# One batch's turned input by transfers, separations on a second engine, last products in two banks, a new order

## The chip, the cores and the metric

The kernel runs on one core of a Trainium2 chip. The core has a matrix engine (TensorE, PE in the profile), a vector engine (VectorE, DVE), an activation engine (ScalarE, ACT), a general engine (GpSimd, POOL), and a sync engine (SyncE, SP) that here only issues DMA transfers. The metric is the device time of one execution in microseconds (us). Lower is better. The time before is the median of three runs.

## The reference

Four batches of 256 rows and 512 columns go through four layers. Cut to what matters:

```python
# L0, x: (4, 256, 512)
w = softmax(x @ router_W.T + router_b)              # (4, 256, 8)
a_sum = einsum('bsh,arh->bsr', x, ctx)              # the context is lora_A
upd = einsum('bsn,bsnh->bsh', w, einsum('bsr,nhr->bsnh', a_sum, lora_B))
x = nan_to_num(x + 0.5 * upd, posinf=1e4, neginf=-1e4)
# L1, cross attention with 32 heads of 16, then a layer norm
Q = x @ Wq.T + bq; K = ctx @ Wk.T + bk; V = ctx @ Wv.T + bv
attn = softmax(where(mask, Q K^T / 4, -inf))
x = layernorm(x + (attn V) @ Wo.T + bo) * ln_g + ln_b
# L2 and L3, each four blocks; the 8 nearest of 512 points from ctx
for i in range(4):
    p = leaky_relu(x)
    x = (w_center[i] p + sum over the 8 neighbours of w_neighbor[i] p) / 9 + x
```

In L2 and L3 both weights are the same matrix, so a block is one product with the weights (`wp`) and one product with a 0/1 matrix that has a one for each neighbour and one for the point itself (`nbr`, four tiles of 128 x 512 for a batch). There are eight such blocks for each batch, one after the other.

## The kernel before

All work of a batch is cut into steps for one engine each. `mixture(b)` is L0, `values(b)`, `queries(b)` and `attention(b, l, ...)` are L1 (`l` is one of the two halves of 128 rows), `nearest(b)` finds the neighbours, and `block(b, i)` is one of the eight blocks. TensorE does all products. A product in full single precision is two instructions in the profile (a transpose is one); in `block` the product `wp` is split into a high and a low part (`wph` by ScalarE at line 1034, `wpl` by VectorE at line 1037), and the product with `nbr` (line 1052) runs over both.

No loop sets the order. The class `Plan` collects every step with an estimated cost, what it reads and writes, and which buffers it needs. `Plan.emit` then plays a list scheduler while the program is built: for each engine it takes, among the steps that could start first (within 0.05 us), the one with the lowest rank. The rank of a step is the due time of its batch (`DEADLINES`) less the length of the work that follows it. A step may have a second engine (`other`); the scheduler takes the one that it thinks ends first. The order found is fixed in the program. Each engine then runs its list in order, and so does the SP queue, where a transfer that waits for its input holds back all transfers behind it. Keys such as `("last", h)` or `after` bind the scheduler alone; what an engine waits for in the run follows from the tiles.

A matmul needs its operand turned, with the contracted dimension on the partitions. `turn(...)` (line 461 and after) does this in two ways. With `by_transfer` false, TensorE transposes four 128 x 128 tiles into a PSUM bank (line 467) and ScalarE copies the bank to SBUF (line 471). With `by_transfer` true, the 32-bit numbers are separated into their upper and lower 16 bits by ScalarE (line 477, tile `..._a`), a DMA transpose issued by SP turns them (line 487, tile `..._t`), and ScalarE or GpSimd joins the halves again (line 495). Three things are turned: `z` (the mixed terms, two for a batch), `x1T` (the updated `x`, two for a batch) and `pT` (the attention weights, eight for a batch). `FROM = 2` says that `z` and `x1T` go by transfer from batch 2 on; `FROM_P = 1` says so of `pT` from batch 1 on.

`mix(b, l, zb)` turns `z`, multiplies it with `lora_BT` (line 523), adds to `x` (line 538), replaces non-finite values (lines 544 to 554), turns the result into `x1T` (line 555), and then adds the bias `bo` to `x` (line 564). The queries of a batch (`q`, line 818) read both halves of its `x1T`. `values` is `v` at line 780.

The loads are issued by SP in the order of the `load...` calls (lines 300 to 324), and they land in that order. `load_xT(3)` is placed in the plan behind the first half of `x1T` of batch 1 (`after`, line 280).

The last block of batch 3 ends in `last(...)`: the second half of its rows is done in two column halves, so that the first half can be added and stored while the second is multiplied. Both column halves are in one PSUM bank, `pb[o]`, and the two additions (line 1107) come after both products (line 1090).

Of the kernel before, what the change touches and what calls it, by code (L numbers as in the profile page):

```python
# [14 lines left out]
ALU = mybir.AluOpType  # L15
# [16 lines left out]
DEADLINES = (0.0, 35.0, 60.0, 67.0)  # L32
# [8 lines left out]
FROM, FROM_P = 2, 1  # L41
# [23 lines left out]
class Plan:  # L65
# [39 lines left out]
    def emit(self, deadline):  # L105
# [16 lines left out]
        while ready:  # L122
# [45 lines left out]
            op.end += op.lag  # L168
# [13 lines left out]
def xattn_seq_kernel(ctx: ExitStack, tc: tile.TileContext, a: dict, out: bass.AP):  # L182
# [106 lines left out]
    def load_k(o):  # L289
        load(("WkT", o), 0.25, lambda: WkT[o], a["WkT"][:, bass.ts(o, H)])  # L290
# [10 lines left out]
    load("cxx2", 0.13, lambda: cxx0[64:128], a["ctx"][0])  # L301
    load("small", 0.05, lambda: consts, a["small"])
    load("ctxT", 0.5, lambda: ctxT.rearrange("p c b v -> p (c b v)"), a["ctxT"])
    load_k(0)
    load_k(2)
    load_points(1)
# [8 lines left out]
    load_x(1)  # L315
    load("rows1", 0.5, lambda: rows1, a["rows1"].partition_broadcast(128))
    load("mask_i", 0.12, lambda: mask_i.rearrange("p b v -> p (b v)"), a["mask"].partition_broadcast(128))
    load_x(2)
    load_w("WoT")
# [141 lines left out]
    def turn(name, by_transfer, src, reads, dst, writes, into=()):  # L461

        if not by_transfer:
# [11 lines left out]
        act(  # L475
            1.08,
            lambda: A_.copy(  # L477
                apart.tile.bitcast(U16).rearrange("p (t n) -> p t n", t=2),
                src().bitcast(U16).rearrange("p (n t) -> p t n", t=2),
            ),  # L480
            reads,
            (apart,),
        )
# [24 lines left out]
    def mix(b, l, zb):  # L508
# [4 lines left out]
            b >= FROM,  # L513
# [5 lines left out]
        for h in range(2):  # L519
# [33 lines left out]
        act(0.63, lambda: A_.activation(odd.tile, v, AF.Identity, bias=zero, scale=0.0), (key, "zero"), (odd,))  # L553
# [3 lines left out]
            b >= FROM,  # L557
# [80 lines left out]
    def nearest(b):  # L638
# [4 lines left out]
        for j in range(H // 128):  # L643
# [11 lines left out]
                0.62,  # L655
# [342 lines left out]
    def block(b, i):  # L998
# [45 lines left out]
        pb = [Buf("bank", f"blk{b}_{i}_{o}") for o in range(NL)]  # L1044

        for m2 in range(2):
            for o in range(NL):

                def gather(m2=m2, o=o):
                    for m in (2 * m2, 2 * m2 + 1):  # L1050
                        for k, part in enumerate(parts[m2]):
                            T_.matmul(  # L1052
                                pb[o].tile,
                                lhsT=part.tile[:, bass.ds(m % 2 * S + o * 128, 128)],
                                rhs=nbr[b, m],
                                start=(m == 0 and k == 0),
                                stop=(m == H // 128 - 1 and k == 1),
                            )

                if (b, i, m2, o) == (B - 1, 2 * NBLK - 1, 1, NL - 1):  # L1060
                    continue
                pe(0.94, gather, (*parts[m2], ("nbr", b, 2 * m2), ("nbr", b, 2 * m2 + 1)), (pb[o],))
        if (b, i) == (B - 1, 2 * NBLK - 1):
            last(b, pb, parts[1], pt)
# [17 lines left out]
    def last(b, pb, parts, pt):  # L1082

        o = NL - 1
        for h in range(2):
            cols = bass.ts(h, H // 2)
            pe(
                0.52,
                lambda cols=cols, h=h: [
                    T_.matmul(  # L1090
                        pb[o].tile[:, cols],
                        lhsT=part.tile[:, bass.ds(m * S + o * 128, 128)],
                        rhs=nbr[b, 2 + m][:, cols],
                        start=False,
                        stop=(h == 1 and m == 1 and k == 1),
                    )
                    for m in range(2)
                    for k, part in enumerate(parts)
                ],
                (*parts, ("nbr", b, 2), ("nbr", b, 3), *pb),  # L1100
                (("last", h),),
            )
        for h in range(2):
# [3 lines left out]
                lambda cols=cols: V_.scalar_tensor_tensor(  # L1107
                    pt[:, o, cols], pb[o].tile[:, cols], 1.0 / (KNN + 1.0), pt[:, o, cols], ALU.mult, ALU.add
                ),
                (pb[o], ("x", b, o), ("last", h)),  # L1110
# [75 lines left out]
```

## Time and profile before

| | |
|---|---|
| median of three runs | 385.94 us (385.63 to 387.9) |
| the profiled execution's own time | 386.5 us |
| its span, first to last instruction | 384.8 us |
| granted TensorE clock | 1.000 |
| TensorE busy | 378.7 us, 98% of the span |
| VectorE busy | 240.0 us, 62% |
| ScalarE busy | 191.3 us, 50% |
| GpSimd busy | 110.3 us, 29% |
| DMA | 25.81 MB, mean 67 GB/s |

The profiled execution took 1.7 us more than its span. Busy time of TensorE counts modelled ends of pipelined matmuls, so 98% says that there is nearly always a matmul under way, not that each runs at its best rate. In a timeline row the first number is the start in us from the beginning of the span and the second how long the group took; then come engine, line, operation, tile written and tiles read, shapes and count; square brackets hold idle time before and who ended it. A row of the groups has the busy time and the mean of one in ns, then the idle time before. A row of the waits has the total in us, how often, and the longest.

### The profile page before, as it was taken

The page shows a single profiled execution, that of the slowest core. Times are in us where ns is not written, and L with a number is a line of the kernel's source. Part 1 is how long each engine was busy: PE and PEld are TensorE (multiplying, and loading weights), DVE is VectorE, ACT ScalarE, POOL GpSimd, SP SyncE. Part 2 cuts the span into 40 slices and gives each one's busy share as a digit, 9 for nine tenths or more (in the row PEclk, how much of TensorE's full clock was granted, in tenths as well). Part 3 has the DMA queues.
Part 4 walks back from the last instruction along what each step waited for, and adds up shares of the span by engine and source line. Part 5 has one row for each costly group of instructions (what it writes and reads, how often), then busy time and mean ns, then how long its engine had stood idle before and what let it go on. Part 6 is the DMA issues. An engine that isn't in the chain of part 4 may idle for free.

```text
span 384.8 us, 5507 instructions
## 1 busy us (share of the span) xinstructions
PE 378.7 (98%) x2120; PEld 291.5 (76%) x2120; DVE 240.0 (62%) x445; ACT 191.3 (50%) x296; POOL 110.3 (29%) x122
## 2 busy tenths in 40 slices
PE   8999999999999999999999999999999999999996
PEld 5848747668887666887867767888888888888885
DVE  1779599995992876955966726535435435435433
ACT  2672755759688769775757722322222221222220
POOL 5483307676356426542054430400000000000000
PEclk9999999999999999999999999999999999999999
DMA  6999500162155305215014610000000001000002
GB/s 201 343 407 348 112 15 1 29 136 42 28 111 112 68 0 110 56 20 90 3 27 89 103 55 2 0 0 2 1 0 2 1 0 56 0 0 2 0 0 111
DMA packets 47386, 25.81 MB, mean 67 GB/s; under 512 B 43200, under 2 KB 43584, under 8 KB 46720
## 3 DMA queue, kind: packets, MB, share of 16 engines
q1 hardware_dynamic: 47360, 25.46, 26.6%
q8 instruction: 17, 0.28, 0.3%
q14 instruction: 9, 0.07, 0.1%
HBM read 12.87 MB, written 2.10 MB: 39 GB/s over the span
## 4 chain that ended last, share of the span: by engine, by line
PE 84%; DVE 9%; DMA 2%; SPq 2%; ACT 2%; issue 1%; DVEq 0%
PE blk L1052 31%; PE wp L1021 29%; PE q L818 7%; PE o L965 5%; PE upd L523 4%; DMA raw<-in_ctx 2%; SPq L273 2%; PE avT L945 2%; PE v L780 1%; PE route L421 1%; PE s L859 1%; DVE rest L649 1%; DVE den L900 1%; DVE s L891 1%; DVE mx L885 1%; DVE top L646 1%
## 5 line engine op out<-in xcount | busy, mean ns | idle before, releaser
L1021 PE MATMUL wp<-fT,p 128*128 128x256 f32 x512 | 120.1, 380 | 0.0
L1052 PE MATMUL blk<-nbr,wph 128*128 128x512 f32 x254 | 110.3, 434 | 0.0
L1021 PEld LDWEIGHTS wp<-fT,p 128*128 128x128 f32 x512 | 96.6, 189 | 17.9 <-issue 2.5
L1052 PE MATMUL blk<-nbr,wpl 128*128 128x512 f32 x254 | 99.6, 392 | 0.0
L1068 DVE SCALAR_TENSOR_TENSOR x<-blk,x 128x512 f32<-128x512 f32 x63 | 42.9, 683 | 69.5 <-PE blk L1052 69.5
L1034 ACT CAST wph<-wp 128x512 fp32r<-128x512 f32 x64 | 37.3, 583 | 94.9 <-PE wp L1021 94.6
L1037 DVE TENSOR_TENSOR wpl<-wp,wph 128x512 fp32r<-128x512 f32 x64 | 43.8, 685 | 37.7 <-ACT wph L1034 37.7
L1052 PEld LDWEIGHTS blk<-nbr,wph 128*128 128x128 f32 x254 | 47.8, 188 | 11.8 <-issue 1.1
L1052 PEld LDWEIGHTS blk<-nbr,wpl 128*128 128x128 f32 x254 | 47.8, 188 | 10.2 <-DVE wpl L1037 0.5
L922 POOL TENSOR_TENSOR s<-s,rden 128x512 f32<-128x512 f32 x32 | 32.6, 1052 | 53.4 <-DVE rden L912 53.4
L1004 ACT ACTIVATE p<-x 128x512 f32<-128x512 f32 x38 | 24.0, 630 | 30.4 <-DVE x L1068 26.6
L477 ACT COPY pT_a<-s 128x1024 uint16<-128x1024 uint16 x24 | 24.6, 1044 | 10.8 <-POOL s L922 6.5
L965 PE MATMUL o<-WoT,avTs 128*128 128x512 f32 x64 | 29.7, 596 | 0.0
L523 PE MATMUL upd<-lora_BT,zTs 128*128 128x512 f32 x64 | 28.8, 597 | 0.8 <-ACT zTs L471 0.8
L818 PE MATMUL q<-x1T,WqT 128*128 128x256 f32 x128 | 29.1, 382 | 0.1
L818 PEld LDWEIGHTS q<-x1T,WqT 128*128 128x128 f32 x128 | 24.0, 190 | 4.0 <-ACT x1T L471 0.6
L523 PEld LDWEIGHTS upd<-lora_BT,zTs 128*128 128x128 f32 x64 | 11.9, 190 | 14.9 <-issue 13.2
L897 ACT ACTIVATE s<-s 128x512 f32<-128x512 f32 x32 | 18.6, 626 | 7.4 <-DVE s L891 7.4
L885 DVE TENSOR_REDUCE mx<-s 128x8 f32<-128x512 f32 x32 | 20.2, 679 | 2.2 <-PE s L859 2.2
L965 PEld LDWEIGHTS o<-WoT,avTs 128*128 128x128 f32 x64 | 11.9, 189 | 11.1 <-issue 10.3
L891 DVE TENSOR_TENSOR s<-s,mx 128x512 f32<-128x512 f32 x32 | 20.2, 678 | 0.0
L900 DVE TENSOR_REDUCE den<-s 128x8 f32<-128x512 f32 x32 | 20.0, 673 | 0.1
(124 smaller groups left out, 415.5 us busy)
## 6 DMA issues: line engine op xcount, KB each, us to landing
xT<-in_xT SPq DMA_DIRECT2D x4, 512.0 KB, 9.7
x<-in_x SPq DMA_DIRECT2D x4, 512.0 KB, 11.2
out<-x SPq DMA_DIRECT2D x7, 256.0 KB, 2.0
WkT<-in_WkT SPq DMA_DIRECT2D x4, 256.0 KB, 6.5
lora_BT<-in_lora_BT SPq DMA_DIRECT2D x1, 1024.0 KB, 9.4
WvT<-in_WvT SPq DMA_DIRECT2D x1, 1024.0 KB, 11.1
rows<-in_rows SPq DMA_DIRECT2D x2, 512.0 KB, 12.3
WoT<-in_WoT SPq DMA_DIRECT2D x1, 1024.0 KB, 11.7
```

What stands on the lines that cost most here:

```text
L477: lambda: A_.copy(apart.tile.bitcast(U16).rearrange("p (t n) -> p t n", t=2), src().bitcast(U16).rearrange("p (n t) -> p t n", t=2),),
L523: T_.matmul(ps2.tile, lhsT=zT.tile[:, bass.ts(c, 128)], rhs=w["lora_BT"][:, c, :], start=(c == 0), stop=(c == NC - 1),)
L818: T_.matmul(ps.tile[:, 0:S], lhsT=w["WqT"][:, c, bass.ts(o, 128)], rhs=x1T[b].tile[:, c, :], start=(c == 0), stop=(c == NC - 1),)
L885: lambda mx=mx, ps=ps: V_.tensor_reduce(mx.tile[:, 0:HPC], heads(ps), AX.X, ALU.max),
L891: lambda mx=mx, ps=ps, s=s: V_.tensor_tensor(heads(s), heads(ps), mx.tile[:, 0:HPC].unsqueeze(2).to_broadcast([128, HPC, V]), ALU.subtract),
L922: lambda s=s, g=g: G_.tensor_tensor(heads(s), heads(s), rden.tile[:, bass.ts(g, HPC)].unsqueeze(2).to_broadcast([128, HPC, V]), ALU.mult,),
L965: T_.matmul(po.tile, lhsT=avT.tile[:, bass.ts(c, 128)], rhs=w["WoT"][:, c, :], start=(c == 0), stop=(c == NC - 1),)
L1021: T_.matmul(ps.tile[:, bass.ts(k, S)], lhsT=p.tile[:, c, bass.ts(2 * m2 + k, 128)], rhs=wi[:, c, :], start=(c == 0), stop=(c == NL - 1),)
L1034: act(0.59, lambda ps=ps, hi=hi: A_.copy(hi.tile, ps.tile), (ps,), (hi,))
L1037: lambda ps=ps, hi=hi, lo=lo: V_.tensor_tensor(lo.tile, ps.tile, hi.tile.bitcast(F32), ALU.subtract),
L1052: T_.matmul(pb[o].tile, lhsT=part.tile[:, bass.ds(m % 2 * S + o * 128, 128)], rhs=nbr[b, m], start=(m == 0 and k == 0), stop=(m == H // 12 ...
L1068: lambda o=o: V_.scalar_tensor_tensor(pt[:, o], pb[o].tile, 1.0 / (KNN + 1.0), pt[:, o], ALU.mult, ALU.add),
```

## The change

- `FROM` is split: `FROM_Z = 2` for `z` as before, `FROM_X = 1` for `x1T`. So both halves of `x1T` of batch 1 are turned by transfers and no longer by TensorE.
- The separation (the first step of a turn by transfer) gets a second engine: ScalarE at an estimated 1.06 us or GpSimd at 1.2 us. This holds for all 34 of them: 24 of `pT`, 4 of `z`, 6 of `x1T`.
- In `last`, the last 128 rows get two banks, `end0` and `end1`, one for each column half. All their products are now done in column halves (16 matmuls of 256 columns, where there were 4 of 512 and 8 of 256), and each addition depends on its own bank.
- The order of the loads: the first quarter of `WkT` and the points of batch 1 come before `ctxT`; the mask and `WoT` come before `rows1`.
- Due times of batches 2 and 3 are 63 and 70 instead of 60 and 67, three estimates of cost are a little different, and a transfer that turns is now taken to land after all loads under way. Estimates and due times change nothing but the order that the scheduler writes.

```diff
-DEADLINES = (0.0, 35.0, 60.0, 67.0)
+DEADLINES = (0.0, 35.0, 63.0, 70.0)
-FROM, FROM_P = 2, 1
+FROM_Z, FROM_X, FROM_P = 2, 1, 1
...
-            op.end += op.lag
+            if op.lag:
+                op.end = max(op.end, self.landed[-1]) + op.lag
...
     load("cxx2", 0.13, lambda: cxx0[64:128], a["ctx"][0])
+    load_k(0)
     load("small", 0.05, lambda: consts, a["small"])
+    load_points(1)
     load("ctxT", 0.5, lambda: ctxT.rearrange("p c b v -> p (c b v)"), a["ctxT"])
-    load_k(0)
     load_k(2)
-    load_points(1)
     load_xT(0)
...
+    load("mask_i", 0.12, lambda: mask_i.rearrange("p b v -> p (b v)"), a["mask"].partition_broadcast(128))
+    load_w("WoT")
     load("rows1", 0.5, lambda: rows1, a["rows1"].partition_broadcast(128))
-    load("mask_i", 0.12, lambda: mask_i.rearrange("p b v -> p (b v)"), a["mask"].partition_broadcast(128))
     load_x(2)
-    load_w("WoT")
...
-        act(
-            1.08,
-            lambda: A_.copy(
+        def split(copy):
+            copy(
                 apart.tile.bitcast(U16).rearrange("p (t n) -> p t n", t=2),
                 src().bitcast(U16).rearrange("p (n t) -> p t n", t=2),
-            ),
+            )
+
+        act(
+            1.06,
+            lambda: split(A_.copy),
             reads,
             (apart,),
+            other=("POOL", 1.2, lambda: split(G_.tensor_copy), True),
         )
...
             f"zT{b}_{l}",
-            b >= FROM,
+            b >= FROM_Z,
...
             f"x1T{b}_{l}",
-            b >= FROM,
+            b >= FROM_X,
...
-    def last(b, pb, parts, pt):
+    def last(b, other, parts, pt):
         o = NL - 1
-        for h in range(2):
+        ends = [Buf("bank", f"end{h}") for h in range(2)]
+        for m2 in range(2):
+            for h in range(2):
...
+                            ends[h].tile[:, 0 : H // 2],
+                            lhsT=part.tile[:, bass.ds(m * S + o * 128, 128)],
+                            rhs=nbr[b, 2 * m2 + m][:, cols],
+                            start=(m2 == 0 and m == 0 and k == 0),
+                            stop=(m2 == 1 and m == 1 and k == 1),
...
-                (pb[o], ("x", b, o), ("last", h)),
+                (ends[h], ("x", b, o)),
```

More of the change, by code (lines that the diff above doesn't have):

```diff
@@ L552, in mix @@
         )
-        act(0.63, lambda: A_.activation(odd.tile, v, AF.Identity, bias=zero, scale=0.0), (key, "zero"), (odd,))
+        act(0.72, lambda: A_.activation(odd.tile, v, AF.Identity, bias=zero, scale=0.0), (key, "zero"), (odd,))
         dve(0.74, lambda: V_.copy_predicated(v, odd.tile.bitcast(I32), hi.tile), (odd, hi), (key,), port=True)
@@ L654, in nearest @@
             act(
-                0.62,
+                0.72,
                 lambda rest=rest, near=near: A_.activation(
@@ L1043, in block @@
             parts.append((hi, lo))
-        pb = [Buf("bank", f"blk{b}_{i}_{o}") for o in range(NL)]
+        pb = [Buf("bank", f"blk{b}_{i}_{o}") for o in range(NL - ((b, i) == (B - 1, 2 * NBLK - 1)))]
         for m2 in range(2):
@@ L1058, in gather @@
                             )
-                if (b, i, m2, o) == (B - 1, 2 * NBLK - 1, 1, NL - 1):
+                if (b, i, o) == (B - 1, 2 * NBLK - 1, NL - 1):
                     continue
@@ L1063, in block @@
         if (b, i) == (B - 1, 2 * NBLK - 1):
-            last(b, pb, parts[1], pt)
+            last(b, pb[0], parts, pt)
         for o in range(NL - ((b, i) == (B - 1, 2 * NBLK - 1))):
@@ L1080, in block @@
                 )
-    def last(b, pb, parts, pt):
+    def last(b, other, parts, pt):
         o = NL - 1
-        for h in range(2):
[L1086 to L1102, printed above, removed]
+        ends = [Buf("bank", f"end{h}") for h in range(2)]
+        for m2 in range(2):
+            for h in range(2):
+                cols = bass.ts(h, H // 2)
+                pe(
+                    0.48,
+                    lambda cols=cols, h=h, m2=m2: [
+                        T_.matmul(
+                            ends[h].tile[:, 0 : H // 2],
[3 more added lines that the diff above has]
+                            stop=(m2 == 1 and m == 1 and k == 1),
+                        )
+                        for m in range(2)
+                        for k, part in enumerate(parts[m2])
+                    ],
+                    (*parts[m2], ("nbr", b, 2 * m2), ("nbr", b, 2 * m2 + 1), *([other] if m2 else [])),
+                    (ends[h],),
+                )
         for h in range(2):
@@ L1106, in last @@
                 0.38,
-                lambda cols=cols: V_.scalar_tensor_tensor(
-                    pt[:, o, cols], pb[o].tile[:, cols], 1.0 / (KNN + 1.0), pt[:, o, cols], ALU.mult, ALU.add
+                lambda cols=cols, h=h: V_.scalar_tensor_tensor(
+                    pt[:, o, cols], ends[h].tile[:, 0 : H // 2], 1.0 / (KNN + 1.0), pt[:, o, cols], ALU.mult, ALU.add
                 ),
-                (pb[o], ("x", b, o), ("last", h)),
+                (ends[h], ("x", b, o)),
                 (("out", h),),
```

## The prediction

> **What bounds the kernel.** I read the page's busy times first, then what TensorE waited for, then its timeline.
>
> ```profile
> PE 378.7 (98%) x2120; PEld 291.5 (76%) x2120; DVE 240.0 (62%) x445; ACT 191.3 (50%) x296; POOL 110.3 (29%) x122
> ```
>
> ```profile
> PE idle L333 <- DVE ones L327: 1.1, 1, 1.1
> PE upd L523 <- ACT zTs L471: 0.8, 1, 0.8
> PE kT L720 <- DMA WkT<-in_WkT: 0.2, 1, 0.2
> ```
>
> TensorE is never seen idle for more than 2.1 us in all. Small waits hide under modelled ends, so I also compared each start with the one before. Beyond the pace of its kind a matmul came 0.94 us late at 20.19 us (`upd`), 0.36 at 9.68 (`kT`), 0.41 at 82.54 (`q`) and 0.33 at 60.67 (`d`): 2.0 us. From 245 us on there is none: eight `wp` and eight `blk` alternate every 3.58 us (1.73 + 1.85). So the time is TensorE's work plus its few waits plus the tail, and a change can win only what it takes from these three. The stretch that the change touches most:
>
> ```profile
> 74.23 5.42 PE L965 MATMUL o<-WoT,avTs 128*128 128x512 f32 x12
> 79.48 1.04 PE L467 MATMUL x1T<-ident,x 128*128 128x128 f32 x8
> 80.45 1.95 PE L780 MATMUL v<-WvT,ctxT 128*64 128x256 f32 x16
> 82.54 7.17 PE L818 MATMUL q<-x1T,WqT 128*128 128x256 f32 x32
> ```
>
> ```profile
> 72.42 1.36 DVE L554 COPY_PREDICATED x<-odd,hi 128x512 f32<-128x512 int32 x2
> ```
>
> ```profile
> 81.43 1.05 ACT L471 COPY x1T<-x1T 128x512 f32<-128x512 f32 x2
> ...
> 93.19 0.64 ACT L1004 ACTIVATE p<-x 128x512 f32<-128x512 f32 x1
> ```
>
> VectorE finishes both halves of batch 1's `x` at 73.78. TensorE is busy with `o` and turns them only at 79.48, 5.7 us later; ScalarE's copies end at 82.48, and `q` starts at 82.54. Every other product then runs until `p` of batch 0 opens the blocks at 93.4. The tail:
>
> ```profile
> 380.03 0.96 PE blk L1090 x8
> 381.02 0.42 DVE x L1107
> ```
>
> ```profile
> 381.02 0.75 DVE L1107 SCALAR_TENSOR_TENSOR x<-blk,x 128x256 f32<-128x256 f32 x2 [0.26 <-PE blk L1090]
> 381.47 0.83 SPq L1116 DMA_DIRECT2D out<-x  x2
> ```
>
> Both column halves are added only after the last product, one after the other.
>
> **Batch 1's turn.** Removed from TensorE: the eight transposes, 80.45 − 79.48 = 0.97 us. Removed from ScalarE: two copies of 0.58. Added for each half:
>
> ```profile
> L477 ACT COPY x1T_a<-x 128x1024 uint16<-128x1024 uint16 x4 | 4.1, 1043 | 1.6 <-issue 1.1 <-DVE x L554 0.4
> L495 ACT COPY x1T<-x1T_t 128x1024 uint16<-128x1024 uint16 x2 | 2.3, 1165 | 0.8 <-DMA x1T_t<-x1T_a 0.8
> L495 POOL COPY x1T<-x1T_t 128x1024 uint16<-128x1024 uint16 x2 | 2.3, 1156 | 0.7 <-DMA x1T_t<-x1T_a 0.7
> ```
>
> that is 1.04 for the separation, 3.2 (median, 3.1 to 4.7) from issue to landing, 1.16 for the join: 5.4 us instead of TensorE's half of 0.97 and a copy of 0.58. On an idle ScalarE the first half (ready at 73.15) would be separated by 74.2 and the second by 75.2; SP issues one transfer each 1.3 us (77.16 to 78.45), so they land near 77.5 and 78.8, and the joins end by 80.0. TensorE, without the transposes, ends `v` at 79.48 + 1.74 = 81.22. So `q` could start at 81.22 instead of 82.54: a gain of 1.32, the 0.97 and most of the wait of 0.41. The cover is 81.22 − 80.0 = 1.2 us; each us beyond it costs one.
>
> The Trainium skill speaks against this move: "VectorE: DVE Perf Modes", Rules for kernel authors, sends a 128 x 128 transpose to TensorE where PSUM will do as its destination, else to the transfer. By the rule one compares 5.4 us with about 1.1 for a half, and if the difference of 4.3 showed the sum would be 4.3 − 0.97 = 3.3 us slower. By the rows 5.7 us lie between the data and their turn on a full TensorE. I take the rows.
>
> What is earned before 93.4 counts only if the blocks can start earlier. GpSimd ended batch 0's `x` at 90.42; ScalarE came to the second `p` (0.64) only at 93.19. So `p` could be there at 91.1, 2.3 us before it was used: room for the gain.
>
> Queues passed: on SP five transposes of the neighbours go out from 69.06 to 80.97, back to back only from 77.16; two more at 74 to 77 fall in the hole, two later ones push three neighbour transposes by 2.5 us, which batch 1 and 2 don't use before 95. The load of batch 3's `xT` (issued 81.02, landed 85.39, used at 89.55) is placed behind the first join, so it may issue 0 to 3 us later; it has 4 us. GpSimd's addition of `bo` now waits for the separation instead of TensorE; its three additions ended at 83.88, and nobody hurried for them.
>
> **Separations on GpSimd.** No row shows one there. The nearest is the join, the same copy of 1024 half-words, 1.16 against 1.17 on ScalarE; so about equal, and a gain only where ScalarE is behind. After 95 us TensorE waits for no turn, so 24 of `pT` moved or not are worth nothing there; hidden by the blocks of the other batches. The other end is contention: GpSimd's cast of `nbr` took 3.78 at 72.98 beside VectorE's two-operand work against 0.61 at 42.94. "SBUF — State Buffer", Who interferes with whom, says that the two share a pair of ports and the later of them stops altogether. By the join's row a separation there costs 1.16; by the rule and the cast's row up to 3.8 if it meets this stretch of VectorE. I take 1.16 for the rest and keep 3.8 for batch 1.
>
> **Last rows.** Sixteen products of 256 columns at 0.12 replace four of 0.231 and eight of 0.12: 1.92 − 1.88 = +0.04. The first addition can start after the fourth last product, near 380.7, behind VectorE's addition that ends at 380.76; the second at 381.06 instead of 381.36. SP's last issue moves from 381.90 to about 381.6. Gain 0.3, less 0.04: 0.25. Bounds: 0, if SP's spacing of 0.43 takes it, and 0.35.
>
> **Loads.** `ctxT` (landed 6.17) gets a quarter of `WkT` (1.21 by the spacing of landings) and points (0.83) ahead of it: about 8.2. `kT` began at 7.51, so up to 0.7 late, unless the products of `csq` (four of 0.37, their input ready at 5.4) fill in. The second quarter lands as before, 9.63, and the wait of 0.36 there goes. Batch 1's points land at 6.3 instead of 10.46, so its distances are ready some 2 us earlier: work for TensorE in the hole of 0.94 at 20.19, and ScalarE's queue is shorter when it should copy `zTs`. The mask lands 1.3 us earlier, and VectorE, which waited 1.0 for it, is free that much sooner for the first `x`. Bounds: +0.7 and −1.3. I take −0.4.
>
> **Due times and estimates.** They move no work. After 95 us ready products are never short, so I take 0; if batches 2 and 3 stopped alternating at the end, a lone block would show its chain (0.59 + 0.69 for the parts, 0.69 + 0.63 for `x` and `p`), some 2 us each time.
>
> **The sum.** The profiled execution took 386.5 with a span of 384.8; −1.3 (turn) − 0.25 (tail) − 0.4 (loads) gives 384.55. The median shown is 0.56 below the profiled execution, so 384.0.
>
> **Rivals.** *All waits go.* The new order takes all 2.0 us of waits, the transposes' 0.97 and the tail's 0.25: 385.94 − 3.2 = 382.7. For it: TensorE has no others. Against: it needs every wait gone and no new one. *The gain is taken back.* TensorE reaches the blocks sooner and waits for batch 0's `p`, because VectorE sets that chain (its windows from 50 to 80 us show 10.00, 10.00 and 9.80 busy of 10); or the separations are never put on GpSimd, since 1.2 is above 1.06, and the part does nothing. Only the tail and a bit of the start remain: 385.5 to 386.5. *The turn comes late (slower).* Place: `q` of batch 1. From 73.2 to 76.65 ScalarE's queue is full, GpSimd's cast is blocked until 76.76; separations end at 77.7 and 78.8, SP is then inside the neighbours' transposes, landings near 82 to 84 with 3.2 to 4.7, joins until 83.3 to 85.5. TensorE is through with `v` at 81.2 and has nothing else (batch 3's `route` waits for its load, which is placed behind this join), so it stands for 2 to 4.3 us, less the 0.97, 0.41 and 0.25: 386.3 to 389; with one blocked separation of 3.8 up to 391. It decides from the point where `q` starts later than 83.2.
>
> **Chances.** Main forecast 0.50 (383.3 to 384.8), all waits go 0.15, taken back 0.20, late turn 0.15. About 1% (3.9 us) is what a measurement can tell here from no change: faster than 382.1 only at the end of the second case, 0.06; slower than 389.8 in about half of the last, 0.08. The range runs from the second case, 382.4, into the last, 387.4.
>
> **What would show it.** Right: eight `x1T` transposes instead of 16; the group of `x1T_t` transfers counts six; `q` of batch 1 follows `v` without a gap, over 1 us sooner; TensorE's busy time about 1 us less; two 256-column additions 0.3 us apart from each other's products. Wrong: TensorE waiting for a join (line 495) or for `p` (line 1004) between 79 and 95 us; a `kT` that waits for `ctxT`; gaps between `wp` and `blk` after 245 us.

## The result

The changed kernel takes 391.62 us, the median of six executions (390.36 to 392.43); the kernel before took 386.72 beside it. The ratio is 1.0129, with a 95% interval of 1.0107 to 1.0150: the change costs 4.9 us. The forecast was 384.0 with a range up to 387.4, so it was wrong in sign. The profiled execution took 391.65 us with a span of 389.5, 4.7 more than before.

The changed kernel's page, its row of busy times and its row of granted clock (40 slices of 9.7 us, tenths of full speed):

```profile
PE 380.5 (98%) x2116; PEld 291.4 (75%) x2116; DVE 242.2 (62%) x445; ACT 181.9 (47%) x285; POOL 118.0 (30%) x133
...
PEclk9999999998999999999999999999999999999999
```

TensorE has eight transposes fewer and four products more (the last rows), and is nevertheless busy 1.8 us longer: something made others take longer. The clock row has one digit below 9, in the slice from 87.6 us. Its waits:

```profile
PE route L422 <- DMA xT<-in_xT: 2.2, 1, 2.2
...
PE o L971 <- ACT avTs L965: 0.8, 1, 0.8
PE upd L529 <- ACT zTs L472: 0.8, 1, 0.8
```

A wait for the load of batch 3's `xT` is new and is the longest of all; a wait of 0.8 for `avTs` is new too; the 0.8 at `upd` is the old one. The stretch in TensorE's timeline that the change touches, and after it the row of the kernel before for `route`:

```profile
79.88 1.95 PE L786 MATMUL v<-WvT,ctxT 128*64 128x256 f32 x16
...
83.01 0.40 PE L635 MATMUL d<-csq,mhalf_r 128*128 128x512 f32 x1
85.56 1.24 PE L422 MATMUL route<-rw,xT 128*128 128x72 f32 x8 [2.15 <-DMA xT<-in_xT]
86.60 8.68 PE L824 MATMUL q<-x1T,WqT 128*128 128x256 f32 x32
```

```profile
89.55 1.90 PE L421 MATMUL route<-rw,xT 128*128 128x72 f32 x16
```

`q` of batch 1 starts at 86.60 instead of 82.54, and it then takes 8.68 instead of 7.17. Between them TensorE stands for 2.3 us (83.24, the paced end of the last `d`, to 85.56) at a `route` that waits for its load, with `q` behind it. Why the joins and the load are late is read on two queues. ScalarE, the separations (line 478) and joins (line 501) of batch 1 with what lies between them:

```profile
73.82 1.05 ACT L478 COPY x1T_a<-x 128x1024 uint16<-128x1024 uint16 x1
74.77 0.58 ACT L965 COPY avTs<-avT 128x512 f32<-128x512 f32 x1
75.25 1.34 ACT L559 ACTIVATE odd<-x,zero 128x512 f32<-128x512 f32 x2
76.56 1.05 ACT L478 COPY x1T_a<-x 128x1024 uint16<-128x1024 uint16 x1
...
80.16 1.15 ACT L501 COPY x1T<-x1T_t 128x1024 uint16<-128x1024 uint16 x1
...
83.01 1.15 ACT L501 COPY x1T<-x1T_t 128x1024 uint16<-128x1024 uint16 x1
```

And SP, which issues all transfers in one order, with its longest wait of this stretch that belongs to these transfers:

```profile
75.04 6.05 SPq L493 DMA_TRANSPOSE x1T_t<-x1T_a  x2
81.15 0.57 SPq L274 DMA_DIRECT2D xT<-in_xT  x1
```

```profile
SPq L493 <- DMA x1T_t<-x1T_a: 3.5, 1, 3.5
```

The second separated tile is there at 77.6, but its transfer is issued only at 79.86, because SP waits 3.5 us for the first transfer itself: the tile that the second one writes was given the buffer that the first one still reads (of the kind `half`, place 3 in the order that the scheduler wrote). The first lands at 79.80, 4.75 us after its issue, the second at 82.91. The load of `xT` is queued behind both, goes out at 81.15 and lands at 85.43. That is nearly as before (81.02 and 85.39), but before it was used at 89.55, after `q`; the new order has that `route` ahead of `q`. Without it `q` would have had its joins at 84.16, later than before as well.

After the pause the clock is halved. The granted clock is the third number from the end of each row (before it come the busy us of each engine in that stretch, after it the DMA share and GB/s):

```profile
84.00:85.00 1.00, 0.00 (x0) 0.00 (x0) 1.00 (x4) 1.00 (x4) 0.52 (x2) 1.00 1.10 325
...
87.00:88.00 1.00, 1.00 (x4) 0.73 (x4) 1.00 (x2) 0.00 (x0) 0.92 (x2) 0.50 0.32 63
...
90.00:91.00 1.00, 1.00 (x6) 0.89 (x5) 1.00 (x3) 0.86 (x2) 0.00 (x0) 1.00 0.00 0
```

From 86.3 to 89.8 us matmuls of `q` stand 0.427 us apart instead of 0.216, which costs some 1.6 us more. Not every execution had this: of the six, two ran at a mean clock of 1.000 and took 390.36 and 390.88, the other four (0.991 to 0.996) took 391.6 to 392.43. The tail, last, came out as forecast: the first addition starts before the last product has ended (385.95).

```profile
385.65 0.77 DVE L1116 SCALAR_TENSOR_TENSOR x<-end,x 128x256 f32<-128x256 f32 x2
...
386.19 0.88 SPq L1125 DMA_DIRECT2D out<-x  x2
```

### The profile page after: what moved, and what is told of

It is laid out like the page before. It is cut to its first block, busy times and chain, and to the rows that moved or that the text cites. A ratio compares the mean times of both kernels' runs of the same rounds, so it can differ in the third digit from the quotient of the medians.

```text
span 389.5 us, 5517 instructions
## 1 busy us (share of the span) xinstructions
PE 380.5 (98%) x2116; PEld 291.4 (75%) x2116; DVE 242.2 (62%) x445; ACT 181.9 (47%) x285; POOL 118.0 (30%) x133
## 4 chain that ended last, share of the span: by engine, by line
PE 80%; DMA 7%; ACT 5%; DVE 2%; SPq 2%; issue 2%; POOL 0%; ACTq 0%
PE blk L1058 28%; PE wp L1027 25%; PE upd L529 7%; PE q L824 7%; PE o L971 4%; DMA pT_t<-pT_a 3%; DMA raw<-in_ctx 3%; PE s L865 2%; SPq L274 2%; PE route L422 1%; PE v L786 1%; DMA xT<-in_xT 1%; PE avT L951 1%; DVE den L906 1%; ACT pT_a L478 1%
## 5 line engine op out<-in xcount | busy, mean ns | idle before, releaser
L1058 PE MATMUL blk<-nbr,wph 128*128 128x512 f32 x252 | 109.0, 433 | 0.0
L824 PE MATMUL q<-x1T,WqT 128*128 128x256 f32 x128 | 30.3, 394 | 0.0
L971 PE MATMUL o<-WoT,avTs 128*128 128x512 f32 x64 | 28.9, 599 | 0.8 <-ACT avTs L965 0.8
L824 PEld LDWEIGHTS q<-x1T,WqT 128*128 128x128 f32 x128 | 25.3, 199 | 3.8
L478 ACT COPY pT_a<-s 128x1024 uint16<-128x1024 uint16 x20 | 20.0, 1043 | 3.1 <-DMA pT_t<-pT_a 1.7
L1016 DVE SCALAR_TENSOR_TENSOR p<-x 128x512 f32<-128x512 f32 x26 | 19.5, 751 | 0.9
```

The source lines that it names most:

```text
L478: copy(apart.tile.bitcast(U16).rearrange("p (t n) -> p t n", t=2), src().bitcast(U16).rearrange("p (n t) -> p t n", t=2),)
L824: T_.matmul(ps.tile[:, 0:S], lhsT=w["WqT"][:, c, bass.ts(o, 128)], rhs=x1T[b].tile[:, c, :], start=(c == 0), stop=(c == NC - 1),)
L971: T_.matmul(po.tile, lhsT=avT.tile[:, bass.ts(c, 128)], rhs=w["WoT"][:, c, :], start=(c == 0), stop=(c == NC - 1),)
L1058: T_.matmul(pb[o].tile, lhsT=part.tile[:, bass.ds(m % 2 * S + o * 128, 128)], rhs=nbr[b, m], start=(m == 0 and k == 0), stop=(m == H // 12 ...
```

## Where the time went, by stage

Small delays hide under modelled ends, so I took each TensorE product's start less the sum of the usual paces of all products before it (a 256-wide one 0.216, a 512-wide one of a block 0.231 and so on), and subtracted the same for the kernel before at the same instant. What is added in each stretch, in us, for one profiled execution of the change and of most kernels that the next section describes:

| kernel | to 30 us | 30–80 | 80–105 | 105–250 | after | work removed | end of TensorE |
|---|---|---|---|---|---|---|---|
| the change | +0.95 | +0.04 | +3.30 | +1.54 | 0.00 | −0.84 | +4.97 |
| load_ahead | +1.90 | +0.15 | +1.29 | +2.20 | 0.00 | −0.84 | +4.70 |
| own_place | +3.52 | +0.40 | +2.96 | +1.68 | +0.02 | −0.84 | +7.71 |
| both_fixes | +1.12 | −0.10 | −0.62 | +1.54 | 0.00 | −0.84 | +1.07 |
| loads_undone | −0.54 | +0.03 | +2.87 | +1.59 | 0.00 | −0.84 | +3.09 |
| best_try | −0.12 | +0.04 | +2.13 | +1.49 | 0.00 | −0.84 | +2.68 |
| turn_act | +0.59 | −0.02 | +1.91 | +2.24 | 0.00 | −0.84 | +3.86 |
| act_only | +1.34 | +0.32 | +1.27 | +0.27 | 0.00 | −0.84 | +2.33 |
| undo_turn | +2.47 | +0.38 | +0.03 | +0.16 | +0.01 | +0.04 | +3.06 |
| late_ctxT | +0.66 | −0.01 | −0.15 | −0.17 | 0.00 | 0.00 | +0.34 |
| last_alone | −0.12 | 0.00 | −0.02 | +0.22 | −0.02 | +0.04 | +0.10 |

(The last column is the sum but for rounding.) With the paces taken a little differently an entry moves by up to 0.3 from one stretch to the next; the last column stays. The span grew by 0.24 less than TensorE's end in the change, which is the tail's gain. The table has one execution of each, and not always a typical one: it is the slowest of own_place, undo_turn and turn_act and the fastest of both_fixes and act_only. The medians of the next section say what it is worth over several.

## The experiments

My theory after the result: batch 1's turn is late because its two transfers go one behind the other, and the load of `xT` behind both, and the pause then costs the clock; a smaller part is lost at the start, by the order of the loads. The rivals: the pause is caused by the load's place alone; the time goes to the separations on GpSimd; the start is no matter. In own_place, load_ahead, warm, both_fixes, late_ctxT, warm_start and best_try the order of every engine is that of the kernel they start from, but for the edit; in the others it is searched anew, though TensorE's came out the same in act_only as in the changed kernel up to 139.9 us, and in turn_act as in loads_undone up to 213.5. `...` marks left-out lines.

### own_place: the second transfer gets a buffer of its own

```diff
-                    k.tile = self.make(k.kinds[0], k.held[0], k.name)
+                    kind, place = ("pT", 0) if k.name == "x1T1_1_t" else (k.kinds[0], k.held[0])
+                    k.tile = self.make(kind, place, k.name)
```

> The changed kernel, its order kept instruction by instruction; only the turned second half of batch 1's x1T is put in a free buffer of pT instead of the one that the first half's separated tile holds. Theory (late turn): the second transfer no longer waits for the first to land, goes out near 77.7 us instead of 79.86 and takes the load of batch 3's xT behind it along; that lands near 83, TensorE's wait of 2.3 us before route falls below 0.5, the granted clock stays at 1.0 there, and the time falls by 3.5 to 4 us to about 387.7. Rival (the transfer's own length, 5.4 us a half, is the cause): the wait moves from route to q and stays above 1.5 us; time above 389.5. Rival (the new order as a whole): no change, 391.

Measured: 390.37 us (388.83 to 394.38), ratio 1.0116 (1.0057 to 1.0175), where about 387.7 was expected. The profiled execution was the slowest of them, with a bad start:

```profile
PE kT L727 <- DMA ctxT<-in_ctxT: 2.8, 1, 2.8
PE wp L1028 <- ACT p L1011: 1.6, 1, 1.6
```

The second transfer goes out at 80.54, right after its separation ends at 80.51, and `route` no longer waits. But TensorE then stands for `p` of batch 0, after which the clock is at 0.50 from 97.4 to 100.8 us, and the median is not separable from the changed kernel's. One wait was removed, and another of nearly its size was behind it.

### load_ahead: the load of batch 3's xT goes out before the first transfer

```diff
+            if op.eng == "SP" and op.bufs and op.bufs[0].name == "x1T1_0_a":
+                self.sent = self.make("xT", 2, "xT3")
+                self.send(self.sent)
...
```

The left-out lines keep `xT3` in that buffer and drop its load at the old place.

> The changed kernel, its order kept, but SP issues the load of batch 3's xT just before batch 1's first turning transfer instead of behind the second. Theory (late turn by way of the SP queue): the load goes out near 73 us and lands before 80, route runs at 83.2 without a wait, and with its 1.8 us TensorE is covered until q's input is joined at 84.2; no drop of the clock; 387.7. Rival (own length of the turn): TensorE waits for the join instead, over 1.5 us, time above 389.5. Rival (order as a whole): 391.

Measured: 391.44 us (387.8 to 392.2), ratio 1.0109 (1.0060 to 1.0158), where 387.7 was expected. The load is issued at 74.26 and lands at 77.93; the wait at `route` and the halved clock are gone, and the gain is gone as well. TensorE's waits:

```profile
PE wp L1031 <- ACT p L1014: 1.5, 1, 1.5
PE kT L730 <- DMA ctxT<-in_ctxT: 1.4, 1, 1.4
```

Why `p` is late, on VectorE, GpSimd and ScalarE:

```profile
87.34 3.44 DVE L561 TENSOR_TENSOR hi<-hi,lo 128x512 f32<-128x512 f32 x2
```

```profile
88.64 1.59 POOL L1001 TENSOR_TENSOR x<-x,rows 128x512 f32<-128x512 f32 x1
```

```profile
91.52 1.04 ACT L482 COPY x1T_a<-x 128x1024 uint16<-128x1024 uint16 x1 [3.62 <-DVE x L564]
...
94.75 0.62 ACT L1014 ACTIVATE p<-x 128x512 f32<-128x512 f32 x1
```

ScalarE has that `p` behind a separation of batch 2, for which it idles 3.62 us, and the `x` that it waits for is late because two additions of VectorE take 1.76 each instead of 0.68. They run beside two additions of GpSimd (87.17 to 90.23, the second one shown), not beside a separation. The changed kernel has the same slow pair at 86.29, hidden there behind the late `q`. This is the rival "the gain is taken back" of the prediction: `q` sooner means the blocks' first `p` is next.

### warm: twenty products without use before the route that waits

```diff
+                    T_.matmul(ps.tile[:, 256:384], lhsT=ones, rhs=ones, start=True, stop=True)
+                    for _ in range(WARM * (b == B - 1 and l == 0))
+                ] + [
```

The products' results are used by nothing.

> The changed kernel, its order kept, with 20 small products of ones (128 columns, results not used) ahead of batch 3's first route product, so that TensorE works through most of its wait for xT. The wait stays. Theory (the idle stretch lowers the granted clock, which then costs on its own): the clock stays at 1.0 after the wait, q runs at 0.216 us a matmul, and the time falls by 1.3 to 1.7 us to about 390.1. Rival (q is slow there for another reason, such as traffic to its operands): the doubled spacing stays, 391.6.

Measured: 390.56 us (390.19 to 391.26), ratio 1.0108 (1.0087 to 1.0129). The clock stays at 1.000 in the profiled execution and the wait shrinks to what the products leave of it:

```profile
PE route L425 <- DMA xT<-in_xT: 0.7, 1, 0.7
```

About 1.1 us less than the changed kernel, a little less than expected: the clock is a part of the loss, not most of it. The two intervals overlap, so the size is not settled, but the changed kernel's own executions with and without the drop of the clock differ by 1.4 on average.

### undo_turn: the change without its turn by transfers

```diff
-FROM_Z, FROM_X, FROM_P = 2, 1, 1
+FROM_Z, FROM_X, FROM_P = 2, 2, 1
```

> The changed kernel with batch 1's x1T turned by TensorE again; all other parts of the change kept, order planned anew. Theory (late turn): no wait for xT or for a join between 79 and 95 us, 16 transposes of x1T, the tail 0.25 us shorter than before, the first 30 us up to 0.9 us longer than before; about 387.2. Rival (loads, due times and the order as a whole are the cause): 390 to 391.

Measured: 389.19 us (389.08 to 389.79), ratio 1.0072 (1.0057 to 1.0088). Leaving the turn out is worth 2.4 us (391.62 − 389.19; 2.2 by the ratios), less than the theory's 4, more than the rival's nothing. Nearly all that is left lies at the start:

```profile
PE kT L726 <- DMA ctxT<-in_ctxT: 2.1, 1, 2.1
```

`kT` then runs at half clock from 10.6 to 14.0. By the table 2.47 of this kernel's 3.06 us are lost by 30 us and next to nothing after 80. So there are two causes, and the wait for `ctxT`, which the loads' order puts there, is the second.

### late_ctxT: the kernel before with only the first loads in the changed order

```diff
...
+    points = lambda: S_.dma_start(out=plan.sent[0:64], in_=a["ctx"][1])
+    small, ctx_t, k0, k2 = (o.fn for o in [o for o in plan.ops if o.load][2:6])
+    plan.issue = {3: k0, 4: small, 5: points, 6: ctx_t, 7: k2}
```

> The kernel before, every engine's order kept; only SP issues its first loads in the changed kernel's order (a quarter of WkT and the points of batch 1 ahead of ctxT). Theory (the late ctxT is the second cause): kT waits for ctxT from 7.4 us to between 8 and 10.5, then for its second quarter of WkT, and where the wait is long the granted clock falls to half for some us; the rest of the trace is as before; the time is 1 to 4 us longer than before, about 389. Rival (the first loads cost nothing, the points that land earlier make up for it): within 0.5 us of before, 386.5.

Measured: 388.35 us (387.18 to 390.0), ratio 1.0045 (1.0031 to 1.0059): +2.0 us (1.7 by the ratio) by this alone.

```profile
PE upd L529 <- ACT zTs L477: 1.0, 1, 1.0
...
PE kT L726 <- DMA ctxT<-in_ctxT: 0.7, 1, 0.7
```

`kT` starts at 8.15 instead of 7.51, and what it loses is not won back at `upd`, which waits 1.0 instead of 0.8. This profiled execution shows only 0.66 us of loss at the start, and 0.34 at TensorE's end; 1.5 more lie in its tail, where the last store takes 3.3 us to land instead of 1.8. While these stores were under way the DMA engines fetched a block of program, which happened in the tail of no other trace:

```profile
q8 instruction: 1, 0.02, 0.8%
...
out<-x SPq DMA_DIRECT2D x2, 128.0 KB, 3.3
```

This execution is a typical one (388.31), so its trace does not show the 2.0 us to be the price of the wait at `kT`: most of it may belong to this tail, which the changed kernel does not have. Better evidence for the loads is the table's first column. The seven kernels with the changed loads lose 0.66 to 3.52 us by 30 us, 1.7 on average; the four with the old ones lie between −0.54 and +0.59. The input itself varies: `ctxT` landed at 7.9 to 9.6 us in the traces with the changed loads and at 6.2 to 7.1 in those with the old.

### loads_undone: turn, second engine and two banks, with loads and due times as before

```diff
-FROM, FROM_P = 2, 1
+FROM, FROM_X, FROM_P = 2, 1, 1
...
+            other=("POOL", 1.2, lambda: split(G_.tensor_copy), True),
...
+        ends = [Buf("bank", f"end{h}") for h in range(2)]
```

> The kernel before with three parts of the change: batch 1's x1T by transfers, separations by ScalarE or GpSimd, the last rows in two banks; loads, due times and estimates as before, order planned anew. Theory (two causes, late ctxT and late turn, adding up): no wait for ctxT in the first 12 us, but the second half's transfer again goes into the first's separated tile and waits for it, so q of batch 1 (now ahead of route) waits for its join 0.5 to 2.5 us; about 388. Rival (the loads are the only cause): 385.5 or less. Rival (the turn is the only cause): as slow as the changed kernel, 390 or more.

Measured: 388.79 us (387.9 to 390.66), ratio 1.0059 (1.0042 to 1.0075): +2.4 us with no wait for `ctxT`.

```profile
PE q L823 <- ACT x1T L500: 1.6, 1, 1.6
PE kT L725 <- DMA WkT<-in_WkT: 1.2, 1, 1.2
```

In this order the `xT` load is in time and `q` waits for the join itself. The two transfers are again one behind the other (74.87 to 78.67, 78.73 to 81.78), and `q` starts at 83.51. Its clock is then halved too:

```profile
85.00:86.00 1.00, 1.00 (x4) 0.74 (x3) 1.00 (x5) 0.17 (x1) 0.92 (x2) 0.50 1.12 214
```

That is some 1.6 of the 2.87 us that the table gives this stretch, and not typical: only two of the 17 executions had a mean clock of 0.996 or less. This and late_ctxT together give 2.4 + 2.0 = 4.4 of the 4.9 us (by the ratios 0.59% and 0.45% of 1.29%); as the place of the 2.0 us is not shown, that the two fit is no proof.

### warm_start: undo_turn with 24 products without use before the first kT

```diff
+                    T_.matmul(ps.tile[:, 0:128], lhsT=ones, rhs=ones, start=True, stop=True)
+                    for _ in range(24 * (o == 0))
+                ] + [
```

> The changed kernel with batch 1's turn undone (as in the run before), and 24 small products of ones ahead of the first kT product, results not used, so that TensorE works through most of its wait for ctxT. Theory (half of what the start costs is the clock that drops after the wait): the wait stays, the granted clock stays at 1.0, kT runs at 0.216 a matmul; 1 to 2 us less than the 389.2 without them, about 387.7. Rival (kT is slow because its weights are still landing): no gain, 389.2.

Measured: 389.94 us (389.58 to 390.86), ratio 1.0083 (1.0053 to 1.0113): no gain over undo_turn. The clock stays at full speed and the time comes back one step later:

```profile
PE upd L529 <- ACT zTs L472: 1.6, 1, 1.6
```

So the halved clock at the start is not what the loads cost.

### best_try: loads_undone with a buffer of its own for the second transfer

```diff
-                    k.tile = self.make(k.kinds[0], k.held[0], k.name)
+                    kind, place = ("pT", 0) if k.name == "x1T1_1_t" else (k.kinds[0], k.held[0])
+                    k.tile = self.make(kind, place, k.name)
```

> As loads_undone, and the turned second half of batch 1's x1T is put in a free buffer of pT. Theory: neither cause is left; the second transfer goes out right behind the first, q waits under 0.5 us, and the 0.97 us of transposes and the 0.25 of the tail are won: 385.0 to 385.7. Rival (TensorE then waits for p of batch 0 instead, gain taken back): 386 to 387.5.

Measured: 389.38 us (387.84 to 391.39), ratio 1.0064 (1.0046 to 1.0083), where under 386 was expected.

```profile
PE kT L726 <- DMA WkT<-in_WkT: 1.6, 1, 1.6
PE q L824 <- ACT x1T L501: 1.3, 1, 1.3
```

The transfers now overlap (75.31 to 78.75, 77.56 to 80.64), and `q` still waits. ScalarE:

```profile
76.47 1.04 ACT L478 COPY x1T_a<-x 128x1024 uint16<-128x1024 uint16 x1
...
81.45 1.03 ACT L478 COPY x1T_a<-x 128x1024 uint16<-128x1024 uint16 x1
82.39 1.16 ACT L501 COPY x1T<-x1T_t 128x1024 uint16<-128x1024 uint16 x1
```

The second half, ready at 73.67, is separated at 76.47, and its join, 1.75 us after the landing, stands behind a separation of batch 2. The buffer was one part of the late turn; ScalarE's order is another, and each alone is enough to hold `q`.

### both_fixes: own_place and load_ahead in one kernel

```diff
-                    k.tile = self.make(k.kinds[0], k.held[0], k.name)
+                    kind, place = ("pT", 0) if k.name == "x1T1_1_t" else (k.kinds[0], k.held[0])
+                    k.tile = self.sent if k.name == "xT3" else self.make(kind, place, k.name)
...
```

> The changed kernel, its order kept, with both: batch 3's xT loaded ahead of batch 1's first transfer, and the turned second half in a free buffer of pT. Theory (the turn is late three times over: shared buffer, SP queue, and ScalarE's own order): the second transfer goes out right after its separation and lands below 3.3 us later, TensorE waits neither for route nor for q; but, as in load_ahead, wp then waits 1 to 2 us for batch 0's p, which ScalarE has behind the separations of batch 2; with the late ctxT still there, 388.5 to 390.5. Rival (the two waits were all of the turn's cost): no wait between 79 and 98 us, 387.5 or less.

Measured: 389.63 us (387.77 to 391.62), ratio 1.0073 (1.0049 to 1.0097). The ten executions lie in two groups, 387.8 to 389.0 and 390.2 to 391.6, and the profiled one is the fastest. In it nothing waits between 79 and 98 us:

```profile
84.23 7.17 PE L829 MATMUL q<-x1T,WqT 128*128 128x256 f32 x32
91.25 1.01 PE L427 MATMUL route<-rw,xT 128*128 128x72 f32 x8
92.09 3.67 PE L1032 MATMUL wp<-fT,p 128*128 128x256 f32 x16
```

TensorE's order is that of the changed kernel, so the two profiled executions can be set against each other product by product: the changed kernel falls 2.3 us behind at `route` and 1.5 more in `q` while the clock is halved, 3.8 of the 3.9 that lie between their ends. By the table the stretch is then 0.62 us ahead of the kernel before, and with the removed work 1.46: the gain that the prediction gave the turn (1.3), once nothing is in its way. It is still slower than before by 1.12 at the start and 1.54 between 105 and 250 us. What makes the slower group is open. It is not the clock, which was 1.000 in four of its five; the wait for `p` of load_ahead would fit, since in the profiled execution VectorE's two additions took 0.68 each and that wait did not come.

### act_only: the change with all separations on ScalarE

```diff
-            other=("POOL", 1.2, lambda: split(G_.tensor_copy), True),
```

> The changed kernel with every separation on ScalarE again (no second engine), order planned anew. Theory (GpSimd's separations cost and gain nothing): 391 to 392, the waits for ctxT and for batch 3's xT as in the changed kernel. Rival (separations on GpSimd hold up VectorE[...], or come late): 389.5 or less. Rival (they are a gain that the rest hides): 393 or more.

Measured: 389.38 us (388.59 to 391.04), ratio 1.0080 (1.0049 to 1.0111). The theory expected no such fall, and the rival "389.5 or less" is met. The two intervals overlap a little, but the two taken together put the difference at 0.49% with 0.37% to either side. The wait for the load is still there:

```profile
PE route L422 <- DMA xT<-in_xT: 2.0, 2, 1.8
```

Product by product up to 139.9 us, the changed kernel loses 0.4 us against this one at `route`, 1.6 in `q`, where its clock is halved and here it is not, and 0.9 at 129.3, its wait for `avTs`, which does not occur here. VectorE, which the rival named, is not relieved: its additions take as long, first here, then in the changed kernel:

```profile
L556 DVE TENSOR_TENSOR hi<-hi,lo 128x512 f32<-128x512 f32 x8 | 7.4, 949 | 0.0
...
L557 DVE TENSOR_TENSOR hi<-hi,lo 128x512 f32<-128x512 f32 x8 | 7.4, 948 | 0.0
```

So the second engine, or the order found with it, has a price in this pair, and contention with VectorE is not shown to be its reason.

### last_alone: the kernel before with two banks at the end

```diff
+        ends = [Buf("bank", f"end{h}") for h in range(2)]
...
-                (pb[o], ("x", b, o), ("last", h)),
+                (ends[h], ("x", b, o)),
```

> The kernel before with one part alone: the last 128 rows in two banks. Theory: from the end of the last product to the end of the span 3.55 us instead of 3.8, TensorE's part 0.04 longer; 0.2 us less than before, 386.1, which is at the edge of what can be told. Rival (SP's spacing takes it): no difference in the profile's tail either.

Measured: 386.5 us (385.5 to 388.12), ratio 0.9995 (0.9979 to 1.0011). The tail from TensorE's end to the end of the span is 3.7 instead of 3.8; a gain of a quarter of a us is below what eleven executions can show, and it is no loss.

### turn_act: the kernel before with the turn and two banks, separations on ScalarE alone

```diff
-FROM, FROM_P = 2, 1
+FROM, FROM_X, FROM_P = 2, 1, 1
...
+        ends = [Buf("bank", f"end{h}") for h in range(2)]
```

> The kernel before with batch 1's x1T turned by transfers and the last rows in two banks, loads and due times as before, and every separation on ScalarE alone; the order is searched anew. Beside loads_undone (388.8) it lacks only GpSimd as a second engine. Theory, the late turn of batch 1 is the cost of this part whichever engine separates: both transfers still come one behind the other, q of batch 1 starts near 83.5 instead of 82.54, and the time is 388 to 389.5. Rival, the cost lies in the separations on GpSimd (VectorE slowed beside them, p and pT late): then without them the time falls to 386 to 387, what the two banks alone took, whatever the turn does.

Measured: 388.23 us (387.36 to 390.11), ratio 1.0041 (1.0025 to 1.0058): +1.6 us. The profiled execution is the slowest one.

```profile
PE q L822 <- ACT x1T L499: 1.5, 1, 1.5
PE kT L724 <- DMA WkT<-in_WkT: 1.0, 1, 1.0
...
PE wp L1025 <- ACT p L1008: 0.7, 1, 0.7
```

Its transfers go out at 76.00 and 79.71 and land at 79.64 and 82.75, one behind the other as in loads_undone, and `q` starts at 84.49. The turn costs its time without GpSimd's help. Loads_undone, which adds the second engine, is 0.6 slower than turn_act, with intervals that overlap. With act_only that makes two pairs of which the kernel without the second engine is the faster, one of them clear of noise: its effect is not shown to be nothing.

## Why the prediction was wrong

**The bound.** Right: TensorE had 2.0 us of waits to win and no slack, so a lost us there is a lost us at the end. I used this for the upper limit of the gain, and too little for the loss: 98% busy also means that later stages take hardly any of a delay back (late_ctxT won back 0.3 after 80 us, and that was the most).

**Batch 1's turn, −1.3: the step that failed** is "the joins end by 80.0", and with it the cover of 1.2 us. Its chain was 1.04 + 3.2 + 1.16 on "an idle ScalarE" with one transfer each 1.3 us. The pieces that the row could give were right: the separation took 1.05 and the join 1.15. What was not in the sum:

- ScalarE was not idle. The second half, ready at 74.88, was separated at 76.56, behind `avTs` and two `odd`: 1.7 us.
- The first transfer took 4.75 us, at the upper end of the range that I had read (3.1 to 4.7), where I took the median. A program fetch was under way (see the end).
- The second transfer waited for the first (79.86 instead of 77.6): 2.3 us. This wait is in no row of the profile of before, since it comes from the buffer that the scheduler gives to the new tile. I had looked at queues and engines and at no buffer.
- The second join ended at 84.16, 4.2 us after my figure, and the cover of 1.2 turned into a wait. What this chain and the pause behind it cost is seen best against both_fixes, 3.8 us in the profiled pair; the medians of the two differ by 2.0.

**The load behind the turn.** I gave it "0 to 3 us later; it has 4 us". It was issued 0.13 later and landed 0.04 later than before, and that was enough, because the new order used it before `q` and not after it: at 85.56 instead of 89.55. The room of a moved transfer is to be read from the new order, which I had taken from the old.

**The rival "the turn comes late"** named this place, the full ScalarE, landings of up to 4.7, joins until 85.5, a TensorE that waits for `route` with nothing else to do, and the point, `q` after 83.2. `q` came at 86.60. I gave it 0.15, since the rows showed 5.7 us between the data and their turn; but those 5.7 us were TensorE's queue, and the new chain stands in ScalarE's and SP's queues instead. Of its price (386.3 to 389, up to 391 with a blocked separation) the mechanism was right and the sum short of two terms, the halved clock (some 1.6) and the loads. The rule that I had weighed, the Trainium skill's "VectorE: DVE Perf Modes", Rules for kernel authors, which prefers TensorE for a 128 x 128 transpose, gave +3.3 for this part. Measured: +1.6 with 1.0 to 2.2 (turn_act, the two banks in it being worth nothing that can be measured); the change less undo_turn gives 2.4. The rule had the sign, the rows as I read them did not.

**Loads, −0.4: the second step that failed.** Its bounds were +0.7 and −1.3. `kT` 0.7 late was in it, and I let the products of `csq` and the hole at 20.19 take it back. They did not: in late_ctxT, which keeps the order, `kT` starts 0.64 later and `upd` 0.66 later (20.85 for 20.19). The sum also took one landing of `ctxT` for all: 8.05 in the changed kernel's trace, near my 8.2, but up to 9.6 in others. The first loads alone cost 2.0 (late_ctxT), of which its own profile shows 0.7 at this place; undo_turn's shows 2.5.

**Last rows, −0.25.** Near in size in the profile (−0.24 from TensorE's end to the end of the span, +0.04 of work), only −0.1 in last_alone's, and too small to measure alone.

**Separations on GpSimd, 0.** Right on the price: seven of the 34 went there, at the same duration as on ScalarE, none of them of batch 1's `x1T`. The effect of 0 is not borne out: without them the time was 2.2 less in act_only and 0.6 less in turn_act. What it left out is that other engines assigned mean another order on ScalarE, where `avTs` came late at 129.3 in the changed kernel and not in act_only. How much is the engine and how much the order is open.

```profile
L478 POOL COPY pT_a<-s 128x1024 uint16<-128x1024 uint16 x4 | 4.2, 1040 | 4.3 <-ACT pT_a L478 4.1
```

**Due times and estimates, 0.** Not run alone. No experiment of a part isolates them, the later loads or the interplay.

The sum as it came out: turn +1.6, first loads +2.0, second engine +0.6 to +2.2, two banks 0, in place of −1.3, −0.4, 0 and −0.25. These parts come from different orders, and the first loads' figure has the doubt named at late_ctxT, so they need not add up to 4.9.

What remains open is what happens between 105 and 250 us. TensorE loses 1.5 to 2.2 us there in seven of the eight kernels with the turn in the table, and 0.2 or nothing in those without it. But these eight have only four orders between them (load_ahead, own_place and both_fixes have the changed kernel's, best_try has that of loads_undone), and act_only, with the turn, loses 0.27; so it is not shown that the turn does it. A good part is single late products: 0.9 us at 129.3 in the changed kernel (`avTs`), 1.0 at 144.0 in loads_undone (`pTs`), 1.0 at 140.1 and 0.9 at 195.8 in turn_act (`wpl`, `p`), where the kernel before has none above 0.4. Why these copies are late there no run took apart.

## What to carry to other kernels

When a step moves from a saturated engine to a chain of copies and transfers, the sum must be made on the queues that it moves to, in the order that they will have: what stands ahead of each copy on its engine, which buffer each transfer writes and who still reads it, and what is queued behind it. Removing one of several equal waits shows the next one (own_place, load_ahead and best_try each removed what they named and gained nothing that could be measured), so the worth of a repair is the difference to the second-latest input. A load that is needed first, such as `ctxT` here, should not be put behind others that are to fill a later hole.

## What the runs showed of the hardware

- **TensorE's clock.** After a pause of 2.3 us in a stream of matmuls the granted clock was 0.50 for 3.4 us (from 86.3 to 89.8), and after a wait of 2.1 at the start of undo_turn likewise. The length of the pause alone does not decide: waits of 1.6 were followed by half clock in loads_undone (84.3 to 87.7) and own_place (97.4 to 100.8), waits of 1.8 in act_only and 1.5 in turn_act were not. In all fourteen traces the changes of the clock lie whole multiples of 3.41 us apart, and of the five stretches at 0.50 ahead of the end four last one of them and one lasts two. At half speed 3.41 us are up to 1.7 us lost (an estimate from these figures). That it matters where a pause falls between two such points would fit and was not tested.
- **A transfer beside a fetch of program.** The first transfer of the change took 4.75 us from issue to landing where the median was 3.2. While it was under way the DMA engines fetched one block of program, on a queue of its own:

```profile
q1 hardware_dynamic: 1056, 0.26, 69.9%
q8 instruction: 1, 0.02, 1.3%
```

  The same transfer took 4.55 in own_place, 4.70 in load_ahead and 5.0 in both_fixes, and 3.8, 3.4 and 3.6 in loads_undone, best_try and turn_act, each with such a fetch beside it. Over all fourteen traces, the 288 transposing transfers of 128x1024 half-words that had neither a fetch nor an ordinary transfer beside them took 3.02 to 3.38 us; of the 156 with a fetch, 81 took more than 3.4, up to 5.28; of the 22 with an ordinary transfer alone, five did, up to 4.72. Stores show it too: 3.3 and 3.4 us in the tail of late_ctxT, the only one with a fetch, and 1.8 to 2.0 in the others. No run moved a fetch away, so this is what goes together and not a tested cause.
- **VectorE beside GpSimd.** The addition of two 128x512 tiles from SBUF took 1.76 us instead of 0.68 in load_ahead, and 1.75 in the changed kernel, beside GpSimd's own additions (1.39 and 1.59 us). In both_fixes it was the other way round: GpSimd's addition took 3.82 us (from 86.14) and VectorE's two 0.68 each (from 86.30).
